# Normalised tokens of five stages made by ScalarE (scale and bias per token) instead of VectorE (subtract, multiply)

## The chip, the cores and the metric

The kernel runs on one core of one Trainium2 chip. Its time is device microseconds of one launch. A core has five engines, each with its own in-order queue: TensorE (PE, with PEld for its weight loads), VectorE (DVE), ScalarE (ACT), GpSimd (POOL) and SyncE (SP, which issues nearly all DMAs here). Engines wait for each other by semaphores.

## What is computed

Four pre-norm transformer layers run one after the other on the same 2048 tokens of 128 features in float32. Each layer has an attention-like and a feed-forward part, and each part reads a layer norm of the running sum.

```python
def _layernorm(x, axis=-1, eps=1e-05):
    m = jnp.mean(x, axis=axis, keepdims=True)
    v = jnp.var(x, axis=axis, keepdims=True)
    return (x - m) / jnp.sqrt(v + eps)

x = x + L0_attn(_layernorm(x));  x = x + L0_ffn(_layernorm(x))   # 16 heads of 8; GELU, 512 wide
x = x + L1_attn(_layernorm(x));  x = x + L1_ffn(_layernorm(x))   # 16 heads of 64; SiLU gate, 384 wide
x = x + L2_attn(_layernorm(x));  x = x + L2_ffn(_layernorm(x))   # 3 neighbours; top-1 of 8 experts
x = x + L3_attn(_layernorm(x));  x = x + L3_ffn(_layernorm(x))   # chunked recurrence; top-2 of 8 experts + shared
```

The running sum is in the reference `x`, in the kernel the on-chip tile `xs`: 16 groups of 128 tokens, with the tokens on the partitions and the 128 features along the row. So the mean and the deviation of a token are one number for each partition.

## The kernel before

**Two phases.** The first, up to about 900 us of the profiled execution, is the attention of layer 0. Beside it run the feed-forward part of layer 0 and the keys and values of layer 1. The second is the attention of layer 1: `l1_attn` goes through 40 units (a block of queries and a pair of heads) of 16 steps. A step has score matmuls into PSUM, two exponentials by ACT into tiles `P`, the sums of the `P` (tiles `acd` on DVE and `acg` on POOL), and, up to two steps later, the value matmuls `P,ka`. A running row maximum for later units is made by `km,qh` matmuls and DVE reductions (`mx<-mi`).

**Background stages.** As soon as attention has finished a block of queries, the rest of the layers for these tokens is put between the steps. For each of 8 blocks of 256 tokens: `stage_a` (feed-forward of layer 1), `stage_a2` and `stage_b` (the three-neighbour attention of layer 2, tiles `kv`, `hb`, `sc`), `stage_b2` (its experts, tiles `gt`, `xb`), and `stage_g` (routing of layer 3's experts). Its experts are 13 hidden tiles for each block, worked off by `s_lane` generators (tiles `t`, `te`, `rwb`, `w3s`). For each of 16 blocks of 128 tokens: `stage_c`, two `chunk`s and `stage_d` (the recurrence of layer 3, tiles `sA` to `sG`, `xst`, `rr`). A chunk needs the state of the chunk before it, so 32 chunks form a single chain through the whole second phase. `s_lane` work is done only when attention has ended; what runs after it is called the tail below.

**Who decides the order.** Every stage is a generator which yields between pieces of work. A planner in the kernel keeps a modelled clock for each engine. After each piece of attention it resumes stages whose inputs should be there by that clock (`Part.may`, `fill`), so the emitted order of every engine is fixed when the kernel is built. Changing an operation's engine changes the modelled clocks and with them the order of everything behind it.

**The layer norm.** `ln_x(c0, n, dst, need, eng)` normalises `n` groups of 128 tokens and transposes them into `dst`. Statistics `mv` (mean, variance) come from two DVE instructions for each group. `vep` is the variance plus 1e-5, `rs` is `vep` to the power of -1/2 by POOL, `xn` is the normalised group, which PE transposes and ACT copies out. With `eng=None` DVE makes `vep` and `xn`:

```python
eng = eng or ve
eng.tensor_scalar(vep[:, :n], mv[:, :n, 1], 1e-5, None, ALU.add)
...
    eng.tensor_scalar(xn[:, i, :], xs[:, c0 + i, :], mv[:, i, 0:1], rs[:, i:i + 1],
                     ALU.subtract, ALU.mult)
```

There are nine call sites. Four of them, in `l0_qk`, `l0_post` and `l0_xp`, pass an engine. Five pass none: `stage_a`, `stage_a2`, `stage_b2` and `stage_g` with n=2 (8 calls each) and `stage_c` with n=1 (16 calls). That makes 48 calls and 80 groups, all of them in the second phase.

Line 147 of the listing is the wrapper through which all recorded operations go, so the profile gives it as the line of nearly everything. Groups are told apart by their tiles.

Of the kernel before, what the change touches and what calls it, by code (L numbers as in the profile page):

```python
# [9 lines left out]
F32 = mybir.dt.float32  # L10
# [3 lines left out]
AF = mybir.ActivationFunctionType  # L14
ALU = mybir.AluOpType
# [55 lines left out]
def body(ctx: ExitStack, tc: tile.TileContext, x, pa, pb, pc, pi, pd, pr, pr0, pe, pw, out):  # L71
# [21 lines left out]
    def tname(v):  # L93
        return getattr(v, "tensor", v).name
# [42 lines left out]
    class Eng:  # L137
# [3 lines left out]
        def __getattr__(self, name):  # L141
            f = getattr(self.e, name)

            def g(*a, **k):
# [7 lines left out]
    te, ve, se, ge, sy = (Eng(e, n) for e, n in ((nc.tensor, "T"), (nc.vector, "D"), (nc.scalar, "A"),  # L152
                                                 (nc.gpsimd, "P"), (nc.sync, "S")))
# [6 lines left out]
    sm = ctx.enter_context(tc.tile_pool(name="sm", bufs=3))  # L160
    tp = ctx.enter_context(tc.tile_pool(name="tp", bufs=2))
# [5 lines left out]
    def take(pools):  # L167
        p = min(pools, key=lambda p: min(bank[p], default=1e9))
        t = PS[p].tile([128, 512], F32, name="mi", tag="mi")
        at = min(bank[p])  # L170
        bank[p].remove(at)
        owner[tname(t)] = p
        rd[tname(t)] = at
        return t
# [3 lines left out]
    def mi():  # L178
        return take(bgpools)
# [6 lines left out]
    def rel(t):  # L186

        n = tname(t)
        bank[owner.pop(n)].append(rd[n] + T["sem"])
# [94 lines left out]
    ident = cst.tile([128, 128], F32, name="ident")  # L284
    make_identity(nc, ident)
    mhalf = cst.tile([128, 4], F32, name="mhalf")
# [3 lines left out]
    xs = cst.tile([128, NT, 128], F32, name="xs")  # L290
# [45 lines left out]
    def ln_x(c0, n, dst, need=0, eng=None):  # L336

        mv = sm.tile([128, 4, 2], F32, name="mv", tag="mv", bufs=5)
        for i in range(n):
            st = sm.tile([128, 6], F32, name="bst", tag="bst")  # L340
            ve.bn_stats(st, xs[:, c0 + i, :])
            ve.bn_aggr(mv[:, i, :], st)
        vep = sm.tile([128, 4], F32, name="vep", tag="vep")
        eng = eng or ve
        eng.tensor_scalar(vep[:, :n], mv[:, :n, 1], 1e-5, None, ALU.add)
        yield
        rs = sm.tile([128, 4], F32, name="rs", tag="rs", bufs=5)
        ge.tensor_tensor(rs[:, :n], vep[:, :n], mhalf[:, :n], ALU.pow)
        if eng is ve:
            yield  # L350
        xn = tp.tile([128, 2, 128], F32, name="xn2", tag="xn2", bufs=4)
        for i in range(n):
            eng.tensor_scalar(xn[:, i, :], xs[:, c0 + i, :], mv[:, i, 0:1], rs[:, i:i + 1],
                             ALU.subtract, ALU.mult)
        yield 1
        t = mi()
        for i in range(n):
            te.transpose(t[:, i * 128:(i + 1) * 128], xn[:, i, :], ident)
        yield
        se.copy(dst, t[:, :n * 128])  # L360
        rel(t)
        yield need
# [188 lines left out]
    def l0_qk(c0, n):  # L551

        w = n * 128
        cols = slice(c0 * 128, c0 * 128 + w)
        yield from ln_x(c0, n, xnT[:, cols], 1, ve if n == 1 else ge)
        ps = mi()
        sides = list(enumerate((("wq", "bq", qd, PARTS["q"]), ("wk", "bk", kd, PARTS["k"]))))
# [212 lines left out]
    def l0_post(c0, n):  # L770
# [3 lines left out]
        for o in range(0, n, 2):  # L774
            yield from wait(("x0", c0 + min(o + 1, n - 1)))
            yield from ln_x(c0 + o, min(n, 2), xt[:, o * 128:min(o + 2, n) * 128], 0, ge)
# [37 lines left out]
    def l0_xp(c0, n):  # L814

        w = n * 128
        i = c0 // 2
        cols = slice(c0 * 128, c0 * 128 + w)
        xn1 = e0w.tile([128, 256], F32, name="xn1", tag="xn1")
        yield from ln_x(c0, n, xn1[:, :w], 0, ve if c0 == 15 else ge)  # L820
        load(xnd[:, cols], xn1[:, :w])
        if c0 != 15:
            if i >= 2:
                yield from wait(("k0", i - 2), ("v0", 2 * i - 4), ("v0", 2 * i - 3))
            pair[i] = [e0w.tile([128, 256], F32R, name=f"xp{k}", tag=f"xp{k}") for k in range(2)]
        xp = [t[:, 128 * (c0 % 2):128 * (c0 % 2) + w] for t in pair[i]]
        se.copy(xp[0], xn1[:, :w])
        yield
        (ve if c0 == 15 else ge).tensor_tensor(xp[1], xn1[:, :w], xp[0].bitcast(F32), ALU.subtract)
        yield  # L830
        emitted.update(("xp", c) for c in range(c0, c0 + n))
# [1289 lines left out]
```

## Time and profile before

| | us |
|---|---|
| median of 3 runs | 2883.26 (2874.99 to 2885.86) |
| the profiled execution | 2863.49 |
| its span | 2861.7 |
| PE busy | 2644.1 (92%) |
| DVE busy | 2223.2 (78%) |
| ACT busy | 1580.9 (55%) |
| POOL busy | 1368.9 (48%) |
| mean granted PE clock | 0.957 |

The span is from the first to the last instruction. A busy PE isn't PE at its peak: its matmuls are pipelined and their ends modelled. In a group's row stand the engine, the operation, the tiles written and read, shapes, the count, then busy time, the mean of one in ns, and the engine's idle time before these instructions with what ended it. A releaser is the instruction which came last among those waited for. The chain is followed back from the last instruction, at each step to its releaser.

The first layer norm with `eng=None` starts at 1261.5 us, the last value matmul of attention at 2507.0 us, and the tail reaches from there to the end. The two stretches used below are 1260 to 2511 us (called "attention") and 2511 to 2862 us ("tail").

### The profile page before, as it was taken

How to read it: one execution, taken by the hardware profiler on the slowest of the kernel's cores; microseconds unless marked ns; L12 is line 12 of the kernel's file. 1: busy time of each engine (PE TensorE's matmuls, PEld its weight loads, DVE VectorE, ACT ScalarE, POOL GpSimd, SP SyncE). 2: the span in 40 equal slices, each digit the busy share in tenths (PEclk: the TensorE clock that was granted, in tenths of full speed). 3: DMA queues.
4: the chain of work that ended last, by engine and by line, in shares of the span. 5: the costliest groups of instructions: out<-in, count | busy, mean ns of one | idle time of the engine just before them, and what ended most of it. 6: DMA issues, size and time to landing. Idle time of an engine off the chain costs nothing.

```text
span 2861.7 us, 50098 instructions
## 1 busy us (share of the span) xinstructions
PE 2644.1 (92%) x16719; PEld 1337.1 (47%) x16719; DVE 2223.2 (78%) x4766; ACT 1580.9 (55%) x4058; POOL 1368.9 (48%) x1599
## 2 busy tenths in 40 slices
PE   6999999999988899999999999999999999888898
PEld 1222232322224444455554544455555566555666
DVE  7899888898733767777777788887878877978775
ACT  1778888887875444444544444444444444434454
POOL 3310110110214677676676776665667556634464
PEclk9999999999988999999999999999999999978798
DMA  6311141230216233443453333333334444322255
GB/s 148 71 33 18 39 118 25 75 88 12 90 35 207 93 117 111 121 122 113 135 144 99 100 102 99 97 103 101 101 102 113 122 121 126 88 54 75 78 134 125
DMA packets 247751, 275.82 MB, mean 96 GB/s; under 512 B 95747, under 2 KB 183330, under 8 KB 247366
## 3 DMA queue, kind: packets, MB, share of 16 engines
q1 hardware_dynamic: 246630, 272.43, 34.8%
q8 instruction: 133, 2.18, 0.3%
q14 instruction: 124, 1.02, 0.1%
q10 hardware_dynamic: 864, 0.20, 0.0%
HBM read 229.97 MB, written 42.28 MB: 95 GB/s over the span
## 4 chain that ended last, share of the span: by engine, by line
PE 62%; DVE 23%; ACT 6%; issue 4%; DMA 3%; POOL 1%; SPq 0%; ACTq 0%; DVEq 0%; POOLq 0%
PE mi L147 62%; DVE mx L147 8%; DVE acd L147 3%; ACT P L147 3%; DVE sB L147 1%; DVE gt L147 1%; DVE xn L147 1%; DVE xs L147 1%; DVE hb L147 1%; DMA rcd<-rc 1%; ACT kf L147 1%; DMA rb<-rcd 1%; DVE sG L147 1%; DVE sc L147 1%; ACT kh L147 1%
## 5 line engine op out<-in xcount | busy, mean ns | idle before, releaser
L147 DVE TENSOR_REDUCE mx<-mi 128x1 f32<-128x512 f32 (+1 forms) x2080 | 1317.7, 681 | 449.2 <-PE mi L147 438.5
L147 ACT ACTIVATE P<-mi 128x512 f32<-128x512 f32 (+3 forms) x2304 | 1119.6, 553 | 854.6 <-PE mi L147 842.6
L147 POOL TENSOR_TENSOR acg<-acg,P 128x512 f32<-128x512 f32 (+3 forms) x800 | 862.3, 1106 | 249.7 <-ACT P L147 249.4
L147 PE MATMUL mi<-P,ka 128*64 128x512 f32 (+3 forms) x2560 | 521.7, 528 | 1.1 <-ACT P L147 1.1
L147 PE MATMUL mi<-qh,ka 64*128 64x512 f32 (+3 forms) x2560 | 480.9, 361 | 18.0 <-DVE mx L147 14.9
L147 PE MATMUL mi<-kop,qop 48*128 48x512 bf16 x1024 | 347.4, 404 | 24.7 <-DVE mx L147 12.3
L147 PE MATMUL mi<-qop,kop 50*128 50x512 bf16 x1024 | 316.5, 389 | 27.3 <-ACT P L147 24.7
L147 PE MATMUL mi<-P,vop 128*32 128x512 f32 x2048 | 303.3, 618 | 13.9 <-ACT P L147 13.9
L147 PEld LDWEIGHTS mi<-qh,ka 64*128 64x128 f32 x2560 | 263.9, 187 | 88.4 <-DVE mx L147 33.6
L147 PE MATMUL mi<-km,qh 64*128 64x512 f32 x1024 | 265.2, 456 | 28.5 <-DVE mx L147 17.8
L147 PEld LDWEIGHTS mi<-P,ka 128*64 128x64 f32 x2560 | 157.7, 138 | 243.1 <-issue 211.4
L147 PE MATMUL mi<-ql,ka 64*128 64x512 f32 (+3 forms) x1280 | 242.0, 352 | 0.0
L147 POOL TENSOR_SCALAR vep<-mv 128x2 f32<-128x2 f32 (+1 forms) x24 | 5.5, 231 | 493.6 <-DVE mv L147 493.6
L147 PE MATMUL mi<-mbt,onr 64*128 64x512 f32 (+3 forms) x1280 | 237.2, 349 | 0.4 <-DMA mbt<-mb 0.4
L147 PEld LDWEIGHTS <-kop 50*128 50x128 bf16 x1024 | 63.5, 95 | 303.2 <-issue 279.6
L147 POOL TENSOR_TENSOR acg<-P 128x512 f32<-128x512 f32 (+3 forms) x80 | 87.5, 1115 | 231.5 <-ACT P L147 133.2
L147 PEld LDWEIGHTS mi<-km,qh 64*128 64x128 f32 x1024 | 115.5, 187 | 174.7 <-DVE mx L147 70.4
L147 PEld LDWEIGHTS mi<-mbt,onr 64*128 64x128 f32 x1280 | 133.3, 187 | 11.3 <-DMA mbt<-mb 1.1
L147 PEld LDWEIGHTS mi<-ql,ka 64*128 64x128 f32 x1280 | 129.6, 188 | 13.7
L147 PEld LDWEIGHTS <-qop 48*128 48x128 bf16 x1024 | 73.0, 95 | 97.4 <-issue 83.0
L147 PEld LDWEIGHTS mi<-P,vop 128*32 128x32 f32 x2048 | 55.6, 109 | 119.3 <-issue 90.4
L147 POOL TENSOR_TENSOR kl<-kf,kh 128x512 f32<-128x512 f32 x32 | 40.9, 1280 | 110.8 <-ACT kh L147 82.3
(510 smaller groups left out, 3484.5 us busy)
## 6 DMA issues: line engine op xcount, KB each, us to landing
ka<-kvd SPq DMA_DIRECT2D x320, 384.0 KB
km<-khd SPq DMA_DIRECT2D x159, 256.0 KB
khd<-kh SPq DMA_DIRECT2D x32, 256.0 KB
kvd<-kh SPq DMA_DIRECT2D x32, 256.0 KB
kvd<-kl SPq DMA_DIRECT2D x32, 256.0 KB
kvd<-vt SPq DMA_DIRECT2D x16, 512.0 KB
w3s<-in_pw_dram SPq DMA_DIRECT2D x37, 192.0 KB
ka<-in_pw_dram SPq DMA_DIRECT2D x36, 192.0 KB
```

What stands on the lines that cost most here:

```text
L147: r = f(*a, **k)
```

## The change

`ln_x` gets a branch of its own for `eng=None`. DVE still makes the statistics. The rest is moved: `vep` to POOL, and `xn` to an ACT activation with the scale `rs` and the bias `nm` = -mean x `rs`, both one number for each token. For `nm` there are two new small instructions, a multiplication by -1 on ACT and a multiplication on POOL. The number of yields is the same.

```diff
-        eng = eng or ve
+        if eng is None:
+
+            nm = sm.tile([128, 4], F32, name="nm", tag="nm")
+            rs = sm.tile([128, 4], F32, name="rs", tag="rs", bufs=5)
+            yield
+            se.mul(nm[:, :n], mv[:, :n, 0], -1.0)
+            ge.tensor_scalar(vep[:, :n], mv[:, :n, 1], 1e-5, None, ALU.add)
+            ge.tensor_tensor(rs[:, :n], vep[:, :n], mhalf[:, :n], ALU.pow)
+            ge.tensor_tensor(nm[:, :n], nm[:, :n], rs[:, :n], ALU.mult)
+            yield
+            xn = tp.tile([128, 2, 128], F32, name="xn2", tag="xn2", bufs=4)
+            for i in range(n):
+                se.activation(xn[:, i, :], xs[:, c0 + i, :], AF.Identity, bias=nm[:, i:i + 1], scale=rs[:, i:i + 1])
+            yield 1
+            t = mi()
+            for i in range(n):
+                te.transpose(t[:, i * 128:(i + 1) * 128], xn[:, i, :], ident)
+            yield
+            se.copy(dst, t[:, :n * 128])
+            rel(t)
+            yield need
+            return
```

## The prediction

> **What bounds the kernel now.** I read the busy times first, then the two stretches in which the changed operation occurs (busy time of each engine by stretch):
>
> ```profile
> PE 2644.1 (92%) x16719; PEld 1337.1 (47%) x16719; DVE 2223.2 (78%) x4766; ACT 1580.9 (55%) x4058; POOL 1368.9 (48%) x1599
> ```
>
> ```profile
> 1260.00:2511.00 1251.00, 1186.63 (x8167) 683.03 (x8167) 1005.93 (x2149) 574.39 (x1717) 799.30 (x899) 0.98 0.38 110
> 2511.00:2862.00 351.00, 300.01 (x1603) 226.09 (x1603) 259.94 (x949) 162.19 (x655) 160.52 (x260) 0.82 0.38 93
> ```
>
> After the stretch and its length come PE, PEld, DVE, ACT and POOL, then the granted clock. PE sets the pace. In attention it is idle for 1251 - 1186.6 = 64.4 us, so nothing that relieves another engine can bring more than that there. DVE is next with 80%; ACT has 54% free. The tail has 51 us of idle PE and a clock of 0.82.
>
> The chain, restricted to attention, puts DVE behind much of what ends last:
>
> ```profile
> by line: PE mi L147 59.1%; DVE mx L147 10.5%; DVE acd L147 4.8%; issue 3.7%; DVE xn L147 1.8%; DMA rcd<-rc 1.8%; DVE hb L147 1.7%; DVE sB L147 1.5%; DMA rb<-rcd 1.4%; DVE xs L147 1.3%; DVE sc L147 1.2%; DVE sG L147 1.0%; DVE gt L147 1.0%; D
> ```
>
> xn, which the change takes from DVE, has 1.8% of 1251 us, or 22.5 us. Next, the groups by shape (1260 us to the end) that price both sides:
>
> ```profile
> L147 DVE TENSOR_SCALAR xn<-xs,mv,rs 128x128 f32<-128x128 f32 x80 | 42.4, 566 | 2.7 <-POOL rs L147 2.6
> L147 ACT ACTIVATE P<-mi 128x256 f32<-128x256 f32 x256 | 82.5, 383 | 112.6 <-PE mi L147 108.1 <-POOL acg L147 2.7 <-POOL xs L147 1.5
> L147 ACT ACTIVATE P<-mi,pcs 128x256 f32<-128x256 f32 x83 | 35.9, 469 | 16.4 <-PE mi L147 16.4
> L147 ACT ACTIVATE en<-e,rr 64x32 f32<-64x32 f32 x32 | 10.2, 318 | 11.0 <-POOL rr L147 10.9
> L147 ACT ACTIVATE j<-e 64x32 f32<-64x32 f32 x32 | 7.2, 225 | 16.7 <-DVE u L147 12.6 <-DVE e L147 3.9
> L147 ACT ACTIVATE oq<-mi 128x128 f32<-128x128 f32 x16 | 4.4, 276 | 4.7 <-PE mi L147 4.5
> ```
>
> Last, one place in the timeline where xn holds PE up:
>
> ```profile
> 1677.50 4.97 POOL L147 TENSOR_TENSOR acg<-acg,P 128x512 f32<-128x512 f32 x4
> 1679.42 1.92 DVE L147 TENSOR_SCALAR xn<-xs,mv,rs 128x128 f32<-128x128 f32 x2
> 1681.39 0.33 PE L147 MATMUL mi<-ident,xn 128*128 128x128 f32 x1 [0.87 <-DVE xn L147]
> ```
>
> Two xn, whose shortest single duration is 0.327 us, take 1.92 us beside POOL additions, and PE stands 0.87 us.
>
> **DVE is relieved.** It loses 80 xn and 48 vep: 31.9 + 7.9 = 39.9 us busy in attention (52 and 31 instructions) and 10.5 + 3.4 = 13.8 us in the tail (28 and 17). How much PE gets of it is bounded for attention. At the least it is the wait that PE and PEld show for xn itself, 1.2 + 2.8 = 4.0 us. At the most it is xn's share of the chain, 22.5 us. In between: the chain has ten clearly visible visits to xn, and in 8 us around each PE was busy 72.7 of 80 us. So 7.3 us of idleness lies there, whatever its cause. I take -7, since behind each of these waits PE itself is next. In the tail only two xn pieces of 0.65 and 0.52 us are among the long ones of the chain. DVE has 107 of its 344 us, so 13.8 x 0.31 = -4; the ends are 0 and -13.8.
>
> **ACT gets 80 activations and 48 small ones.** No row has a pointer for both scale and bias. 128x128 without either took 276 ns (oq). A bias tile added 469 - 383 = 86 ns at 128x256, a scale tile 318 - 225 = 93 ns at 64x32. Estimate: 276 + 86 + 93 = 455 ns; the ends are 276 and, with one step more for reading SBUF, 550. The small one is like the 64x2 activation ce<-cc, 202 ns. Sum: 52 x 0.455 + 31 x 0.202 = 29.9 us in attention, 28 x 0.455 + 17 x 0.202 = 16.2 us in the tail. Behind them stand the exponentials, and PE waits for those. In attention PE and PEld waited 2.3 + 42.2 = 44.5 us for P with 574 us of ACT work. In proportion 29.9 us more make +2; the ends are 0 (P is used up to two steps later) and +30.
>
> The page "ScalarE: Activation LUTs" of the Trainium skill (Rules for kernel authors) speaks against the change: for additions and multiplications it says to use VectorE, not ScalarE. By the shortest xn, 327 ns, that holds here (ACT would cost 128 ns more, 10 us over 80). By the busy time over all, 42.4 us / 80 = 530 ns, ACT is cheaper. "SBUF — State Buffer" (two separate sides) gives a reason: VectorE in a 2-port mode and GpSimd share a port pair, and the later one is blocked for a whole instruction. The 1.92 us above fits that, though no run here shows it as the cause.
>
> **The new wait.** nm on ACT waits for DVE's mv, with exponentials or lane activations queued behind it; xn on ACT waits for POOL. Until now POOL was the one that waited for DVE, at rs for vep: 33.3 us in 21 waits, 12.0 of it in attention, and lost little. If ACT stands as long, the cost is between 0 and +33.3. In attention the single waits were 2.4 us at most, which two steps of P cover. In the tail, with 21.3 us, ACT is idle for 189 of 351 us. I take a fifth of those 21.3: +4. In the built order xn follows its own nm directly in four of 48 cases, most often with some instructions between.
>
> **POOL** gets vep (231 ns, from the 24 of the first phase) and a 128x2 multiplication (between the 196 ns of a 128x2 copy and the 264 ns of a 64x32 multiplication). 48 x (0.231 + 0.264) = 23.8 us, of which 15.3 lie in attention, where POOL has 452 us free. 0; without that cover +15. PE matmuls, the copy to dst and all DMAs stay as they are in number, so SP's queue only shifts.
>
> **The order.** The planner reorders from the first changed layer norm on, at 1261 us. Before that nothing changes. Comparing the built orders after the last P,ka: stage_b has two blocks left instead of one, stage_b2 three instead of two, stage_c eight instead of seven, stage_g seven instead of eight; lanes and chunks are equal. Mostly this work only moves from attention to the tail. But there the clock is 0.82 and not 0.98, and the next chunk must wait for its stage_c, where before it could start at once. The moved block is worth about 9 us of PE and, by 16 expert sums of 0.347, a reciprocal of 1.74 and four scans of about 0.5, over 9 us of DVE. The ends are 0 and +18; I take +5.
>
> **Sum:** -7 - 4 + 2 + 4 + 0 + 5 = 0 us. The profiled execution took 2863.5 us, 19.8 less than the median 2883.3. Put on the median, the forecast is 2883 us.
>
> **Rivals.**
> - *DVE's relief goes to PE in full*: -22.5 in attention and -13.8 in the tail, ACT's +2 and the order's +5 and little else: -29, or 2854 us. For: DVE's 32% of the chain, stretched xn. Against: PE has only 7.3 us idle around xn's ten visits.
> - *ACT becomes the late one* (slower): it stands at nm and xn as POOL stood at rs, and what's behind it is late in all 33.3 us: -11 + 2 + 33 + 5 = +29, 2912 us. Place: lane activations and recurrence in the tail, exponentials in attention. It decides once a single stand is longer than the two steps by which P runs ahead. For: in-order ACT feeds nearly every PE operand. Against: the short waits of POOL in attention.
> - *The tail starts late* (slower): the 16 chunks left spread over about 253 us, 16 us each. If the recurrence is one chunk later and the moved PE work comes on top: -11 + 2 + 4 + 25 = +20, 2903 us. For: the counts above. Against: lanes fill PE meanwhile.
>
> **How the numbers follow.** A change of 0.5%, 14 us, is about what can be told from none. Forecast 0.39, full relief 0.28, late ACT 0.19, late tail 0.14. The forecast is read as within 14 us; the first rival is faster, the other two slower. So faster 0.28, same 0.39, slower 0.33. The range takes in the full relief and the late ACT with a few us beyond each: 2848 to 2918.
>
> **What would show it.** Right: xn on ACT of 0.45 us each, DVE some 50 us less busy after 1260 us, attention shorter by about 10 to 25 us and the tail longer by as much, PE waits for xn and P as small as before. Wrong towards faster: idle PE in attention far under 60 us with a tail that isn't longer. Wrong towards slower: ACT waits for mv or nm of several us with PE waits for P beside them, or a tail beyond 375 us with PE idle over 60. Wrong altogether: a first phase which isn't the same.

## The result, and the profile after

The changed kernel takes 2899.46 us (median of 5, 2898.68 to 2908.86) against 2874.99 us (median of 5) for the kernel before: a ratio of 1.0082, interval 1.0054 to 1.011. It is 24 us slower, where no change was forecast.

The profiled execution after took 2899.46 us. That of before, 2863.49 us, is faster than every other run of its kernel (72 runs of it between 2866 and 2895 us came with the experiments), so the two profiles differ by 36 us instead of 24. I use them for places and mechanisms, and the ratios of the timed runs for sizes.

Busy times of the whole execution after, then its two stretches (here attention ends at 2521 us, 4 us after the last value matmul, as 2511 us did before; same columns):

```profile
PE 2663.9 (92%) x16719; PEld 1352.7 (47%) x16719; DVE 2180.0 (75%) x4636; ACT 1615.2 (56%) x4190; POOL 1394.2 (48%) x1697
```

```profile
1260.00:2521.00 1261.00, 1186.49 (x8133) 685.40 (x8130) 965.41 (x2018) 592.15 (x1776) 815.11 (x956) 0.97 0.39 110
2521.00:2898.00 377.00, 319.51 (x1636) 238.97 (x1635) 256.78 (x949) 179.08 (x728) 170.18 (x300) 0.79 0.31 82
```

DVE is relieved, by 44 us: 1222 us busy after 1260 us instead of 1266 (some 50 were forecast). Yet attention is 10 us longer although work has moved out of it, with 74.5 us of idle PE instead of 64.4, and the tail is 26 us longer, in this pair of traces.

The moved instructions, by shape from 1260 us on, have about the forecast price (xn 492 ns against 455, nm 202 against 202):

```profile
L147 ACT ACTIVATE xn<-xs,nm,rs 128x128 f32<-128x128 f32 x80 | 35.9, 492 | 3.9 <-POOL nm L147 3.8
L147 ACT ACTIVATE nm<-mv 128x2 f32<-128x2 f32 x32 | 6.5, 202 | 3.2 <-DVE mv L147 3.1
L147 POOL TENSOR_TENSOR nm<-nm,rs 128x2 f32<-128x2 f32 x32 | 7.7, 242 | 26.4 <-ACT nm L147 25.1
```

The waits that the last column names are small on ACT: 3.8 us for POOL at xn, 5.0 us in all for DVE at nm. The 31 us that POOL stands for ACT's nm (25.1 here, the rest with the 128x1 shape) replace the 33 us that it stood for vep. PE's weight loads waited 38.4 us for P in attention, against 42.2 before. ACT did not become the late engine.

In the chain, restricted to attention, xn isn't among the named lines any more:

```profile
by line: PE mi L147 62.0%; DVE mx L147 9.5%; DVE acd L147 5.7%; issue 3.1%; DVE sB L147 2.3%; DMA rcd<-rc 2.2%; DMA rb<-rcd 2.1%; DVE o L147 1.6%; DVE hb L147 1.1%; DVE sc L147 1.0%; DVE xs L147 1.0%; DVE sG L147 0.9%; ACT P L147 0.6%; DVE 
```

So the instructions cost about what was said, and the time seems to be lost elsewhere; the experiments below test that. Two places show how. The first is the start of the tail, in PE's timeline (only `P,ka`, the last matmul of stage_c, and the first one of a chunk). Before:

```profile
2505.83 1.52 PE L147 MATMUL mi<-P,ka 128*64 128x256 f32 x8
2507.28 0.29 PE L147 MATMUL mi<-kf,xst 32*32 32x64 f32 x2
```

After:

```profile
2516.10 1.52 PE L147 MATMUL mi<-P,ka 128*64 128x256 f32 x8
2520.36 0.44 PE L147 MATMUL mi<-sC,kf 32*64 32x64 f32 x4
2535.68 0.29 PE L147 MATMUL mi<-kf,xst 32*32 32x64 f32 x2
```

Chunk 17 begins right behind attention before. After, the stage_c that it needs is only being finished in the tail, and the chunk begins 18.4 us behind the last value matmul's start, 28.4 us later than before. From there both kernels look alike: 16 chunks in 263 and 270 us, then 92 us to the end.

The second is one gap out of several in attention. PE, DVE and POOL in the timeline of the kernel after, around 2470 us, and PE, PEld, DVE, ACT, POOL and granted clock in 10 us stretches:

```profile
2473.86 0.42 PE L147 MATMUL mi<-w2n,ef 32*64 32x32 f32 x2 [5.49 <-DVE e L147]
```

```profile
2468.44 5.14 DVE L147 TENSOR_TENSOR acd<-P 128x256 f32<-128x256 f32 x2
2473.50 0.20 DVE L147 TENSOR_TENSOR ef<-mi,v2f 32x64 f32<-32x64 f32 x1
2473.64 0.17 DVE L147 TENSOR_TENSOR e<-mi,kvt 64x32 f32<-64x32 f32 x1
```

```profile
2468.59 0.71 POOL L147 TENSOR_TENSOR xs<-xs,prs 128x256 f32<-128x256 f32 x1
2469.28 1.39 POOL L147 TENSOR_TENSOR acg<-acg,P 128x256 f32<-128x256 f32 x2
2470.64 0.28 POOL L147 TENSOR_TENSOR acs<-at,ce 64x64 f32<-64x64 f32 x1
2470.89 2.07 POOL L147 TENSOR_TENSOR acg<-acg,P 128x256 f32<-128x256 f32 x3
```

```profile
2460.00:2470.00 10.00, 8.37 (x88) 5.68 (x87) 8.74 (x15) 4.96 (x21) 9.83 (x16) 1.00 0.69 154
2470.00:2480.00 10.00, 6.14 (x38) 3.79 (x38) 5.26 (x12) 2.18 (x8) 6.02 (x10) 0.66 0.26 87
```

The order puts a sum of P ahead of the chunk's error `e` on DVE. Such an addition mostly takes about 0.41 us. Here the first of the two lasts 4.81 us, until POOL has finished a run of back-to-back instructions. PE waits 5.49 us for `ef` and `e`; before, the same matmul of the same chunk (the 15th, at 2460.9 us) waited 0.51 us. Half clock is granted from 2470.8 us, in the middle of the wait, for 6.8 us, which makes the 0.66. So this neighbourhood costs twice, once by the wait and again by the clock. The next large gap, at the end of attention, is one of 4.55 us behind DVE too:

```profile
2507.62 0.41 PE L147 MATMUL mi<-m__31374,en 64*32 64x64 f32 x2 [4.55 <-DVE m__31374 L147]
```

**An account that closes.** From the trace, take PE's busy time from 1260 us to the end, count the part under half clock by half, and call it work. The rest of the stretch is idle time, and what half clock cost (half of the busy time under it). In us:

| kernel | work | idle | lost to half clock | sum |
|---|---|---|---|---|
| before | 1410.8 | 115.1 | 75.8 | 1601.7 |
| after | 1406.6 | 131.4 | 99.4 | 1637.4 |
| changed instructions, old order | 1405.8 | 110.0 | 82.0 | 1597.8 |
| old instructions, new order | 1405.6 | 137.5 | 113.1 | 1656.1 |

Work is the same within 6 us. The difference between before and after, 35.6 us, is idle PE (+16.3) and half clock (+23.6), with 4.3 us less work. The last two rows are the first two experiments.

A row is a single execution. The kernel of the hold experiment below, for example, has the old order up to 2358 us and got there 11 us later than the trace of before. The larger gaps repeat better. In attention, gaps of PE longer than 1.2 us went from 16 with 29.6 us to 23 with 51.8 us, and every one of them ended with DVE. In the traces of all four kernels that keep the old order through attention (before, the first experiment, the old plan in attention, and vep on DVE, all below) such gaps sum to 29.6 to 36.3 us; in the three with the new order (after, the old instructions in the new order, and the new plan in attention) to 49.6 to 51.9 us. The gap in front of this chunk's `w2n,ef` is 5.5 us in all three. So these 13 to 22 us belong to the order, whichever instructions stand in it.

### The profile page after: what moved, and what is told of

The parts are those of the page before. It is cut to its first block, busy times and chain, and to the rows that moved or that the text cites. A ratio compares the mean times of both kernels' runs of the same rounds, so it can differ in the third digit from the quotient of the medians.

```text
span 2897.4 us, 50204 instructions
## 1 busy us (share of the span) xinstructions
PE 2663.9 (92%) x16719; PEld 1352.7 (47%) x16719; DVE 2180.0 (75%) x4636; ACT 1615.2 (56%) x4190; POOL 1394.2 (48%) x1697
## 4 chain that ended last, share of the span: by engine, by line
PE 50%; DVE 19%; issue 3%; ACT 3%; DMA 3%; POOL 1%; SPq 0%; POOLq 0%; DVEq 0%; ACTq 0%
PE mi L147 50%; DVE mx L147 5%; DVE acd L147 4%; ACT P L147 1%; DVE sB L147 1%; DMA rcd<-rc 1%; DMA rb<-rcd 1%; DVE xs L147 1%; DVE o L147 1%; DVE gt L147 1%; DVE hb L147 1%; DVE sG L147 1%; DVE sc L147 1%; DVE P L147 1%; ACT kf L147 0%
## 5 line engine op out<-in xcount | busy, mean ns | idle before, releaser
L147 POOL TENSOR_SCALAR vep<-mv 128x2 f32<-128x2 f32 (+1 forms) x72 | 17.4, 241 | 524.2 <-DVE mv L147 513.1
L147 POOL TENSOR_TENSOR kl<-kf,kh 128x512 f32<-128x512 f32 x32 | 40.9, 1279 | 110.8 <-ACT kh L147 82.4
```

What stands on the lines that cost most here:

```text
L147: r = f(*a, **k)
```

## The experiments

The theories: *order* (the planner, told other engines and prices, emits another order of stages, and that costs) against *instructions* (a longer layer norm and more work in ACT's in-order queue cost). `note` is the call by which the planner is told of an operation; calls through `nc` go past it.

**Changed instructions at the old places.**

```diff
+            note("D", "tensor_scalar", (vep[:, :n], mv[:, :n, 1]), {})
...
-            se.mul(...); ge.tensor_scalar(vep ...); ge.tensor_tensor(nm ...); se.activation(xn ...)
+            nc.scalar.mul(...); nc.gpsimd.tensor_scalar(vep ...); nc.gpsimd.tensor_tensor(nm ...); nc.scalar.activation(xn ...)
+                note("D", "tensor_scalar", (xn[:, i, :], xs[:, c0 + i, :], mv[:, i, 0:1], rs[:, i:i + 1]), {})
```

> The changed instructions (vep and nm on POOL, nm and xn on ACT) put at the places that the planner gave to the old ones: it is told the old costs. PE's order is the old one, instruction by instruction. Theory order (the new order of the stages costs the 24 us, the instructions nothing or a little less than nothing): 2860 to 2876 us against 2875 before, half-clock time as before. Theory instructions (a longer layer norm and a blocked ACT queue cost it, whatever the order): 2893 to 2905 us, with longer PE waits for xn and P than before.

2864.25 us, ratio 0.9949 (0.9928 to 0.997), as the order theory expected: faster than before by half a per cent. Its stretches:

```profile
1260.00:2513.00 1253.00, 1190.19 (x8165) 687.49 (x8161) 980.62 (x2065) 597.58 (x1798) 814.12 (x960) 0.98 0.38 110
2513.00:2858.00 345.00, 297.63 (x1605) 222.91 (x1604) 249.05 (x905) 174.73 (x701) 168.63 (x295) 0.82 0.39 94
```

ACT has as much to do as in the changed kernel, and here it even stands 20 us for POOL at xn. Still the tail is 32 us shorter than after.

**Old instructions in the new order.**

```diff
+            nc.vector.tensor_scalar(vep[:, :n], mv[:, :n, 1], 1e-5, None, ALU.add)
...
-            se.mul(...); ge.tensor_scalar(vep ...); ge.tensor_tensor(nm ...); se.activation(xn ...)
+            note("A", "mul", ...); note("P", "tensor_scalar", ...); note("P", "tensor_tensor", ...)
+                nc.vector.tensor_scalar(xn ...); note("A", "activation", ...)
```

The planner is told of an `nm` that is only a name and a shape here; nothing is computed for it.

> The old instructions (vep and xn on DVE), emitted in the order that the planner makes for the changed kernel: it is told the new costs. PE's order is that of the changed kernel, instruction by instruction. Theory order: 2893 to 2910 us, like the changed kernel or above it since DVE is not relieved. Theory instructions: 2870 to 2882 us, like the kernel before.

2923.1 us, ratio 1.0148 (1.0123 to 1.0173), slower than the changed kernel itself, as the order theory allowed, though beyond its 2910 us.

```profile
1260.00:2530.00 1270.00, 1189.78 (x8126) 685.64 (x8122) 1001.73 (x2100) 570.11 (x1689) 797.72 (x891) 0.97 0.38 109
2530.00:2917.00 387.00, 328.87 (x1633) 246.12 (x1632) 267.20 (x990) 168.87 (x686) 164.44 (x268) 0.77 0.30 79
```

The four kernels make a square, and both of its sides agree. The order costs 1.0148 with the old instructions and 1.0082 / 0.9949 = 1.0134 with the changed ones. The instructions are worth 0.9949 in the old order and 1.0082 / 1.0148 = 0.9935 in the new one. The theory of instructions has fallen; they help by some 15 to 19 us. The addition of 4.81 us described above stands in this kernel too (2475.7 us, 4.81 us), and neither in the kernel before nor in the one with the old order. Long DVE instructions as such are no mark of the new order, though: those of over 2 us in attention sum to 23.8 us before, 32.4 in the first experiment, 26.9 after and 19.9 here. What differs is where they stand.

**Two other orders of the old instructions.** The planner is told that POOL's power takes 0.4 us longer in these layer norms, or that xn costs DVE nothing:

```diff
+        if bare: clk["P"] += 0.4; wr[tname(rs)] += 0.4; piece[0] += 0.4      # the first, after the power
+            if bare: clk["D"] = at                                            # the second, after each xn
```

> All instructions as before; only the planner is told that POOL's power takes 0.4 us longer in these 48 layer norms, so the stages are placed a little later. Theory order: the time moves by over 0.5% (15 us or more) though no instruction is added or moved to another engine, as any new order here can. Theory instructions: within 8 us of before.

2876.0 us, 0.999 (0.9976 to 1.0005).

> All instructions as before; only the planner is told that xn costs DVE no time, as if DVE had been relieved without anybody else being loaded. Theory order: the time moves by over 0.5% in one direction or the other. Theory instructions: within 8 us of before.

2890.23 us, 1.0027 (1.0012 to 1.0043). Both missed the "over 0.5%" that the order theory expected of any new order. A later layer norm alone or a freer DVE alone in the plan doesn't make the bad order; a new order isn't always a bad one.

**Is it the late chunk?** In the changed kernel the recurrence ends 35 us later than before (2770.2 to 2805.3 us), and the end follows 92 us behind in both. That suggested that the late chunk 17 explains nearly all. I held only its stage_c in the kernel before:

```diff
             yield from wait(("b", b3 // 2), ("d", b3 - 4))
+            if b3 == 8:
+                yield from wait("tail")
...
+    emitted.add("tail")                       # when attention has ended
```

> The kernel before with one more wait in the planner: stage_c of the ninth block of 128 tokens (number 8) may start only when attention has ended, so chunk 17, the first of the tail, can't start right behind the last value matmul as it does before; in PE's order it stands 64 matmuls behind it. Every instruction is as before. Theory late recurrence (the tail ends a fixed time after the recurrence, so the 24 us are the late start of chunk 17): 2900 to 2920 us, chunk 17 some 30 to 40 us after the last value matmul, about 92 us from the end of the recurrence to the end. Theory gaps (the new order costs by more idle PE and half clock spread over attention): within 10 us of before, since the order up to stage_c 8 is the old one.

2889.36 us, 1.0039 (1.0023 to 1.0054). Chunk 17 began 40.9 us behind the last value matmul, more than twice the changed kernel's 18.4. But from the end of the recurrence to the end it took 65.5 us instead of 91.5, since 29 lane tiles (hidden tiles of layer 3's experts) instead of 44 were left: lanes had used the time in which the recurrence stood, the hole. So a late chunk costs, but 12 us where I expected 25 to 45, and a little over the 10 of the gap theory. In the changed kernel the hole is filled by the stage_b, stage_b2 and stage_c work moved there, and 43 lane tiles are left at the end of the recurrence.

**Is it cured by an earlier stage_c?** Three more orders of the changed instructions:

```diff
-order="hdmBbAaEcCeg"
+order="hdmBbcCAaEeg"
```

> The changed kernel with both stage_c generators asked ahead of stage_a and stage_a2 by the planner (order hdmBbcCAaEeg). 17 chunks stand before the last value matmul and the next one right behind it; chunk 17 isn't late. Theory late recurrence: 2850 to 2872 us. Theory gaps: no reason for less, 2885 to 2905 as in the changed kernel.

2895.41 us, 1.0058 (1.0039 to 1.0077). Chunk 18, here the first of the tail, started at once, but the 15 chunks left took 20.5 us each instead of 16.4.

```diff
-                d = 0.3 + 0.16 * cols
+                d = 0.3 + 0.16 * cols if k_op(a, k) else 0.2      # k_op: not a multiplication
...
+                clk["A"] += 0.2                                   # before each xn
```

> The changed kernel, with the planner told measured prices: 0.2 us for POOL's small multiplication instead of 0.62 (128x2), and 0.43 for xn on ACT instead of 0.23. 18 chunks stand before the last value matmul, the next 24 matmuls behind it. Theory late recurrence: 2845 to 2870 us, if attention isn't longer by more than the two chunks save (two times 16 us). Theory gaps: 2880 to 2905.

2885.26 us, 1.0024 (1.0009 to 1.004). True prices make the best of these three orders, 0.6% better than the changed kernel's, but not the old one. One run can't tell whether the prices did that or the luck of another order.

```diff
-order="hdmBbAaEcCeg"
+order="hdmcCBbAaEeg"
```

> The changed kernel with stage_c asked ahead of stage_b too (order hdmcCBbAaEeg). 19 chunks stand before the last value matmul, but stage_b lies back, and the chunk after the next stands 201 matmuls into the tail. Theory late recurrence: the chunks won are lost again at that place, 2870 to 2900 us; if only the number of chunks left counted, 13 instead of 16, it would be 2835 to 2855 us. Theory gaps: 2880 to 2905.

2898.27 us, 1.0062 (1.004 to 1.0084): 13 chunks left, 21.7 us each. The late recurrence as the only cause has fallen. Against the changed instructions in the old order (0.9949) these three lose 1.1%, 0.75% and 1.1% in different places.

**Where in the order?** The plan is told the old costs in one phase and the new ones in the other. PE's order is exactly the old, or the new one, up to the end of attention.

```diff
+            old = not tail        # first kernel;  second kernel: old = bool(tail)
...                                # if old: the calls of the first experiment, else those of the changed kernel
```

> The changed instructions; the planner is told the old costs until attention has ended and the new ones from there. PE's order is the old one through attention and leaves it only in the tail. If the new order costs mainly in attention and by what it leaves for the tail: 2858 to 2872 us, near the kernel with the old plan throughout (2864). If the new costs make a bad order in the tail itself: 2880 to 2900.

2885.61 us, 1.0018 (0.9999 to 1.0037).

> The changed instructions; the new costs until attention has ended, the old ones from there. PE's order is that of the changed kernel through attention. If the order of attention and what it leaves is what costs: 2892 to 2908 us, like the changed kernel, with chunk 17 about 18 us behind the last value matmul. If the order within the tail costs: 2865 to 2880.

2895.99 us, 1.0052 (1.0035 to 1.0069). Each is in the range in which its own half of the order costs, so my either-or missed: both halves do. With the changed instructions throughout: old and old 0.9949, old then new 1.0018, new then old 1.0052, new and new 1.0082. The new attention order with what it leaves costs 0.64 to 1.03%, the new order of the tail 0.3 to 0.69% (the 0.3 alone would lie within the two intervals).

**vep left on DVE**, otherwise as in the first experiment:

```diff
-            note("D", "tensor_scalar", (vep[:, :n], mv[:, :n, 1]), {})
+            ve.tensor_scalar(vep[:, :n], mv[:, :n, 1], 1e-5, None, ALU.add)
```

> As the kernel with the changed instructions at the old places, but vep stays on DVE as before; POOL gets the multiplication for nm alone. PE's order is the old one. If the gain of the instructions comes from xn leaving DVE (42 of the 54 us): 2860 to 2868 us, ratio to before 0.993 to 0.997. If vep leaving DVE matters: nearer to before, 2870 to 2878.

2875.28 us, 0.9981 (0.9962 to 1.0001): the median lies in the range in which vep matters. PE's order is the old one, yet its runs spread from 2863 to 2889 us, and the interval overlaps that of the first experiment. How the gain of the instructions divides between xn and vep stays open.

The version that beats both kernels is the first experiment, the changed instructions in the old order.

## Why the prediction was wrong

- **DVE's relief (-7 and -4), ACT's work (+2), the new wait (+4), POOL (0).** Together -5; measured -15 to -19 in both orders. Direction right, size too small by a factor of three to four. The relief was put at the idle time around xn's ten visits alone (two of those stretches overlap by 3 us, which changes nothing: 7.2 us idle of 77). That it also saves half clock isn't shown: with the new order the changed instructions have 6.1 us less idle and 13.6 less half clock, with the old one 5.1 less idle and 6.2 more half clock. The prices held: xn 492 ns (455, ends 276 and 550), nm 202, POOL's vep 253 and multiplication 242 (231, and 196 to 264). The end of 33 us for ACT's new wait, on which the rival *late ACT* stood, wasn't approached: ACT stood 8.8 us, and 26.2 in the first experiment (19.9 at xn, 6.3 at nm), which was faster than before all the same.
- **The order (+5, ends 0 and +18).** This is the step that failed; it is worth +38 to +43. It priced what crosses the boundary to the tail (9 us of PE, 9 us of DVE, a waiting chunk) and took the rest of the order for equal, because counts at the boundary were nearly equal. The runs show three things in its place: more gaps inside attention (13 to 22 us in those over 1.2 us), where the order makes PE stand behind DVE; a worse order within the tail (0.3 to 0.69%); and a later chunk, of which a hole of 41 us cost 12 us in the hold experiment.
- **The clock.** I read 0.98 and 0.82 as properties of the two stretches, and called the 64.4 us of idle PE the most that attention could give; 21.6 us more went to half clock there. In attention they go with the gaps: in the traces before and after, each of the 9 and 12 stretches of half clock begins inside a PE gap of 1.1 to 5.5 us or within 2 us behind it. But not every gap brings one, in the tail some begin without a gap, and there is no fixed price: against before, 16.3 us more idle came with 23.6 us more half clock in the changed kernel, 20.1 with 4.7 in the plan with a free xn, and 1.6 with 24.7 in the hold experiment.
- **The rival *tail starts late*** came near in time (2903 us), by chance, and had its place right: chunk 17, 28 us later. Its price wasn't: the tail grew by 26 us, not by a chunk of 16 plus 9 us of work as such, but by several causes together, and attention grew by 10. The 2899 us lie inside the stated range too, and that is luck as well: its upper end stood for a late ACT, which didn't come.
- **What I said would show it**: "attention shorter by about 10 to 25 us and the tail longer by as much" is refuted on the first half. "A tail beyond 375 us" came true, with 57 us of idle PE instead of over 60.

What stays open is which property of the plan makes an order bad. Of the orders tried with either set of instructions none beat the old one by more than its interval. No single price given to the planner explains the loss. Nor is it shown whether the old order is good because the planner's constants suit it or merely by luck.

## What to carry to other kernels

When a scheduler places the work, moving an instruction to a freer engine is two changes, and the new order can be worth more than the instruction: here +38 to +43 us against -15 to -19. Separate them before judging: emit the new instructions while the planner is told the old costs, and the other way round. And look at the granted clock behind each PE gap: a gap can cost more than its length, though how much more isn't fixed.

## What was not expected of the hardware

- A DVE addition of two SBUF tensors, mostly 0.41 us, took 4.81 us beside seven POOL instructions that followed each other without a break. The Trainium skill, "SBUF — State Buffer" (two separate sides), says that a VectorE instruction with two SBUF inputs and a GpSimd instruction that reads SBUF contend for a shared port pair, which the first one holds for its whole instruction. The trace fits such a lock; if it is one, DVE can stay out for several POOL instructions in a row, not only one. No run here took the POOL work away to prove it.
- Half clock is granted in the traces only for stretches of 3.4 us and multiples of it (3.413, 6.827, 10.240 and so on up to 34.1 us), but for the last stretch of each execution. The Trainium skill, "TensorE: Matmul & The Clock Gate" (the HAM clock gate), describes such a window and the half rate after idleness; here gaps of PE as short as 1.1 us went with it. Over the whole span half clock cost (half of PE's busy time under it) 105 us before and 129 us after, 3.7% and 4.5%.
